# Written order in all of pass 1 of a two-layer graph kernel, with operand calls in two batches of three

## Chip, cores and metric

The kernel runs on one core of a Trainium2 chip. Its time is the device time of one execution in microseconds (us): median 2493.08 of three runs (2492.97 to 2498.91). A core has five engines that run side by side: TensorE (PE in the profile, with its weight loads as PEld) for matrix products into PSUM, VectorE (DVE), ScalarE (ACT) and GpSimd (POOL) for work on rows of elements, and SyncE (SP), which here issues transfers. Each works through its own queue of instructions and waits for semaphores of the others.

## What is computed

Two graph layers over 128 graphs of 64 nodes with 768 features each. Pass 1 of the kernel is layer 0; pass 2, an attention layer, is not touched by the change.

```python
# --- layer 0 ---
h = relu(layernorm(x))                              # x: 128 x 64 x 768
ctx  = (adj   @ (h @ Wadj.T)) / max(deg, 1)         # adj: 0/1, 64 x 64 per graph
ctx += (adj.T @ (h @ Wrev.T)) / max(rdeg, 1)
ctx += h @ Wself.T                                  # biases left out here
rel  = agg  @ Wr.T      # agg[i]  = sum over j of adj[i,j] * E[rels[i,j]]
rel += ragg @ Wrr.T     # the same over the transposed graph
x = x + ctx + rel
# --- layer 1: (graph attention), input relu(layernorm(x)) ---
```

## The kernel before

The 8192 rows are worked through as 32 pairs (p) of 128-row tiles (k = 0, 1). The three weight products of layer 0 are joined into one 3 x 3 block product, done for pairs 1 to 31 with 15 instead of 18 (as in fast matrix multiplication), so sums of blocks have to be formed: `form` makes sums f1 to f11 of the operand blocks a00 to a12, and `weights_sums` sums g and u, v, w of the weight blocks, once. Each product has 6 matmuls (12 instructions, since f32 goes in two), and its PSUM bank a, b, c or d is read by VectorE after it:

```python
PRODUCTS = (       # operand, weight, bank, first in bank, block of x, sign, with counts
    ("f1", "g6", "a", True, "11", "+", False),
    ("f7", "g10", "b", True, "00", "-", False),
    ("a01", "b11", "d", True, "01", "+", True),
    ("f4", "b21", "a", False, "01", "-", False),
    ("a00", "g12", "b", False, "01", "-", False),
    ("f3", "g8", "c", True, "12", "-", False),
    ("a02", "g14", "a", False, "00", "-", False),
    ("f9", "g9", "b", False, "02", "+", False),
    ("f11", "b10", "d", True, "00", "+", True),
    ("f6", "g5", "a", False, "02", "+", False),
    ("f8", "g3", "b", False, "12", "-", False),
    ("f10", "b12", "c", False, "02", "+", True),
    ("f5", "b22", "a", False, "12", "-", False),
    ("a11", "g1", "b", False, "11", "+", True),
    ("f2", "g11", "a", False, "10", "+", True),
)
...
psw = px.enter_context(tc.tile_pool(name="psw0", bufs=1, space=bass.MemoryType.PSUM))  # pwa to pwd
pss = px.enter_context(tc.tile_pool(name="pss0", bufs=2, space=bass.MemoryType.PSUM))  # pb: two
...
            def product(an, bn, b, first, c, sign, cnt):
                def step(q, s):
                    if first and q == s == 0:
                        new(b)                       # bank[b] = psw.tile([P, 512], F32, name=f"pw{b}")
                    nc.tensor.matmul(bank[b][:, :CQ], OPS[p, an][:, q, s, :], bw[bn][...], ...)
                    if q == KQ - 1 and s == 2 and c:
                        if cnt:
                            counts(b, c)             # two bf16 matmuls on the table of relations
                        add(b, c, sign)              # VectorE: x += or -= bank
                ...                                  # 6 steps a product
            for x in PRODUCTS if p else PLAIN:       # 90 steps a pair
                product(*x)
            rest_of = ["12"] if p else ["00", "10"]  # counts alone, bank d, and its add
```

What the next pair needs is made beside the products of this one: `merged(main(p), side)` puts each side step ahead of the product step whose number it has. `operands` makes one operand block: 4 matmuls (8 instructions, 64 rows each) into a `pb` buffer of two banks, one for each graph of the tile, and a copy to SBUF. `count_t` turns the counts of relations by TensorE, through the same `pb` buffers.

```python
        def count_t(p, k):
            ...
            for i, (a, b) in enumerate(PARTS):
                nc.tensor.transpose(pn[: 3 * (b - a), i, :], ..., identb)
                nc.scalar.copy(cn[: 3 * (b - a), i, :], pn[: 3 * (b - a), i, :])

        def operands(p, k, q):
            t = 2 * p + k
            ps = pss.tile([P, GT, 512], F32, name="pb")
            for i in range(2):
                kb = 2 * q + i
                for g in range(GT):
                    s = slice(g * N, (g + 1) * N)
                    nc.tensor.matmul(ps[:, g, i * 3 * N : (i + 1) * 3 * N],
                                     H0[t][s, kb * P : (kb + 1) * P],
                                     rts[p % 2][s, k].rearrange("p s n -> p (s n)"), ...)
            a = OPS[p, f"a{k}{q}"] = ...             # SBUF, 128 x 768 f32
            nc.scalar.copy(a.rearrange("p h s (g n) -> p g (h s) n", g=GT),
                           ps[:, :, : 6 * N].rearrange("p g (x n) -> p g x n", n=N))
```

The side steps, with the engine that has most of the work: `prep`, `prep_c`, `ids_worth`, `ids_sum`, `digits` (VectorE: the counts of relations), `devs` or `deviation` (VectorE: mean and variance, then a power on GpSimd), `degrees` (one matmul) with a reciprocal and two products on VectorE, `finish` (the end of the pair before: statistics; then mean, ScalarE's relu, GpSimd's sum, three stores), `load` (SyncE).

Up to and with pair 1's stretch the instructions of each engine are kept in the order in which the program writes them (`manual_schedule`, in the variable `written`). For pairs 2 to 31 they are not: the tile scheduler places them.

```python
        second = [                                   # beside pair 1, for pair 2
            (0, lambda: form(1, "f5", "f6", "f3")), (7, lambda: prep(2)),
            (7, lambda: weights_sums("g9")), (10, lambda: form(1, "f10")),
            (13, lambda: devs(2)), (18, lambda: form(1, "f11")),
            (20, lambda: degrees_and_norms(2)), (25, lambda: weights_sums("g1")),
            (30, lambda: prep_c(2)), (32, ends[0]), (37, lambda: ids_worth(2, 0)), (40, ends[1]),
            (43, lambda: ids_sum(2, 0)),
            (46, lambda: operands(2, 1, 2)), (46, lambda: operands(2, 1, 1)),
            (49, ends[2]), (53, lambda: form(2, "f1")), (55, ends[3]),
            (56, lambda: ids_worth(2, 1)),
            (58, lambda: operands(2, 0, 0)), (58, lambda: operands(2, 0, 2)),
            (61, lambda: ids_sum(2, 1)), (64, lambda: digits(2)),
            (66, lambda: form(2, "f7", "f4")), (66, lambda: load(3)), (74, row_constants),
            (70, lambda: operands(2, 1, 0)), (70, lambda: operands(2, 0, 1)),
            (77, lambda: form(2, "f8", "f9", "f2")),
            (80, lambda: count_t(2, 0)), (85, lambda: count_t(2, 1))]
        for p in range(NP):
            if p < 2:
                more = (first, second)[p]
            else:                                    # own: f5 f6 f3, f10, f11; side: as above
                more = own(p) + side(p + 1) + [(3, ...finish(p - 1, k)...)]
            if p == NP - 1:
                more += fetch()                      # weights of pass 2: loads and sums
            merged(main(p), more)
            if p == 1:
                written.close()
```

Of the kernel before, what the change touches and what calls it, by code (L numbers as in the profile page):

```python
# [8 lines left out]
F32 = mybir.dt.float32  # L9
# [6 lines left out]
P = 128  # L16
# [116 lines left out]
def kernel(  # L133
# [45 lines left out]
    nc = tc.nc  # L179
# [56 lines left out]
            step()  # L236

    in_order = {mybir.EngineType.PE, mybir.EngineType.DVE, mybir.EngineType.Activation,  # L240
                mybir.EngineType.Pool}
    written = ctx.enter_context(ExitStack())
# [33 lines left out]
                a = c * HB + i * H  # L276
                nc.sync.dma_start(dl[a : a + H, :], ident[0:H, 0:H])

    def deviation(src, to, mv, behind=False):

        st = small.tile([P, 2, 6], F32, name="st")
        for i in range(2):
            ins = nc.vector.bn_stats(st[:, i, :], src[:, i * HALF : (i + 1) * HALF])  # L283
            if behind and i == 0:
                tc.keep_in_program_order(ins)
        nc.vector.bn_aggr(mv, st.rearrange("p a b -> p (a b)"))
        ve = small.tile([P, 1], F32, name="ve")
        nc.vector.tensor_scalar(ve, mv[:, 1:2], EPS, None, op0=OP.add)  # L288
        nc.gpsimd.tensor_tensor(to[:, 0:1], ve, mhalf, op=OP.pow)  # L289

    def scaled_mean(to, mv):

        nc.vector.scalar_tensor_tensor(to[:, 1:2], mv[:, 0:1], -1.0, to[:, 0:1],
                                       op0=OP.mult, op1=OP.mult)

    def stats(src, to, behind=False):
        mv = small.tile([P, 2], F32, name="mv")
        deviation(src, to, mv, behind)
        scaled_mean(to, mv)

# [59 lines left out]
    with ExitStack() as px:  # L362
# [126 lines left out]
        def relu(t, to):  # L489
            h = H0[t] = work.tile([P, D], F32, name="h0")  # L490
            nc.scalar.activation(h, X[t], AF.Relu, scale=to[:, 0:1], bias=to[:, 1:2])

        def norm(t):
            to = small.tile([P, 2], F32, name="rn")
            stats(X[t], to, behind=(t // 2 == 3))
            relu(t, to)

        def prep(p):

            af = ADF[p] = work.tile([P, 2, 2, N], F32, name="af", bufs=1)  # L500
            ins = nc.vector.tensor_copy(af, AI[p])
            if p == 3:
                tc.keep_in_program_order(ins)
            ab = AB[p] = work.tile([P, 2, 2, N], BF16, name="ab", bufs=1)
            nc.vector.tensor_copy(ab, af)

# [21 lines left out]
        def degrees(p):  # L528


            ds = pss.tile([P, 2, 512], F32, name="pb")[:, 0, : 4 * N].rearrange(
                "p (k d n) -> p k d n", k=2, d=2)
            nc.tensor.matmul(ds, blkb, AB[p], start=True, stop=True)
            rd = work.tile([P, 2, 2, N], F32, name="rd", bufs=1)
            nc.vector.tensor_scalar(rd, ds, 1.0, None, op0=OP.max)
            return rd

        def one_over(rd):
            nc.vector.reciprocal(rd, rd)

        def over_degrees(p, rd):

            for d in range(2):
                nc.vector.tensor_mul(rts[p % 2][:, :, 1 - d, :], ADF[p][:, :, d, :], rd[:, :, d, :])
# [16 lines left out]
        def count(p, k):  # L561
            ids_worth(p, k)
            ids_sum(p, k)
# [17 lines left out]
        def count_t(p, k):  # L581
            c3 = CT_T[p, k]
            pn = pss.tile([P, 2, 512], F32, name="pb")[:, 0, :P].bitcast(BF16).rearrange(
                "p (i n) -> p i n", i=2)
            cn = CT_T[p, k] = work.tile([P, 2, P], BF16, name="cntT", bufs=4)
            for i, (a, b) in enumerate(PARTS):
                nc.tensor.transpose(pn[: 3 * (b - a), i, :],  # L587
                                    c3[:, a:b, :].rearrange("p v c -> p (v c)"), identb)
                nc.scalar.copy(cn[: 3 * (b - a), i, :], pn[: 3 * (b - a), i, :])

        def operands(p, k, q):


            t = 2 * p + k
# [7 lines that stand above are left out]
                                     rts[p % 2][s, k].rearrange("p s n -> p (s n)"),  # L602
                                     start=True, stop=True)

            a = OPS[p, f"a{k}{q}"] = (
                work.tile([P, KQ, 3, P], F32, name="oq") if (k, q) == (1, 1) else
                work.tile([P, KQ, 3, P], F32, name="op", bufs=17))
            nc.scalar.copy(a.rearrange("p h s (g n) -> p g (h s) n", g=GT),  # L608
                           ps[:, :, : 6 * N].rearrange("p g (x n) -> p g x n", n=N))

        def form(p, *names):

# [72 lines left out]
            mv = small.tile([P, 2], F32, name="mv")  # L685
            return (lambda: deviation(X[t], to, mv), norm_and_store)

        def degrees_of(p):
            rd = degrees(p)
            one_over(rd)  # L690
            over_degrees(p, rd)

        def side(p):

            if p >= NP:
                return []
            return [(24, lambda: load(p + 1)),
                    (0, lambda: (prep(p), prep_c(p))),
                    (0, lambda: norm(2 * p)),
                    (0, lambda: norm(2 * p + 1)),  # L700
                    (9, lambda: degrees_of(p)),
                    (15, lambda: count(p, 0)),
                    (30, lambda: count(p, 1)),
                    (40, lambda: digits(p)),
                    (46, lambda: operands(p, 1, 2)),
                    (46, lambda: operands(p, 1, 1)),
                    (51, lambda: form(p, "f1")),
                    (58, lambda: operands(p, 0, 0)),
                    (58, lambda: operands(p, 0, 2)),
                    (64, lambda: form(p, "f7", "f4")),  # L710
                    (70, lambda: operands(p, 1, 0)),
                    (70, lambda: operands(p, 0, 1)),
                    (76, lambda: form(p, "f8", "f9", "f2")),
                    (80, lambda: count_t(p, 0)),
                    (80, lambda: count_t(p, 1))]

        def own(p):

            return [(0, lambda: form(p, "f5", "f6", "f3")),
                    (10, lambda: form(p, "f10")),  # L720
                    (18, lambda: form(p, "f11"))]

        def deviations(ts):
# [40 lines left out]
        def weights_sums(*names):  # L766
# [16 lines left out]
            (23, lambda: prep(1)),  # L783
            (24, lambda: devs(1)),
            (26, lambda: table_part(2)),
            (28, lambda: degrees_and_norms(1)),
            (30, lambda: weights_sums("w", "v")),
            (36, lambda: weights_sums("g6")),
            (38, lambda: weights_sums("u", "g14")),
# [18 lines left out]
            (91, lambda: form(1, "f8", "f9", "f2")),  # L808
            (92, lambda: count_t(1, 1))]

        ends = [f for k in range(2) for f in finish(0, k)]
        second = [
            (0, lambda: form(1, "f5", "f6", "f3")),
            (7, lambda: prep(2)),
            (7, lambda: weights_sums("g9")),
            (10, lambda: form(1, "f10")),
            (13, lambda: devs(2)),
            (18, lambda: form(1, "f11")),
            (20, lambda: degrees_and_norms(2)),
            (25, lambda: weights_sums("g1")),  # L820
            (30, lambda: prep_c(2)),
            (32, ends[0]),
            (37, lambda: ids_worth(2, 0)),
            (40, ends[1]),
            (43, lambda: ids_sum(2, 0)),
            (46, lambda: operands(2, 1, 2)),
            (46, lambda: operands(2, 1, 1)),
            (49, ends[2]),
            (53, lambda: form(2, "f1")),
            (55, ends[3]),  # L830
            (56, lambda: ids_worth(2, 1)),
            (58, lambda: operands(2, 0, 0)),
            (58, lambda: operands(2, 0, 2)),
            (61, lambda: ids_sum(2, 1)),
            (64, lambda: digits(2)),
            (66, lambda: form(2, "f7", "f4")),
            (66, lambda: load(3)),
            (74, row_constants),
            (70, lambda: operands(2, 1, 0)),
            (70, lambda: operands(2, 0, 1)),  # L840
            (77, lambda: form(2, "f8", "f9", "f2")),
            (80, lambda: count_t(2, 0)),
            (85, lambda: count_t(2, 1))]
        for p in range(NP):
            if p < 2:
                more = (first, second)[p]
            else:
                more = own(p) + side(p + 1) + [
                    (3, lambda: [f() for k in range(2) for f in finish(p - 1, k)])]
            if p == NP - 1:  # L850
                more += fetch()
            merged(main(p), more)
            if p == 1:
                written.close()


    with ExitStack() as px:
# [432 lines left out]
```

## Time and profile before

| | |
|---|---|
| time, median of 3 runs | 2493.08 us |
| span of the profiled execution, granted TensorE clock | 2493.3 us, 0.996 |
| pass 1, first product to last counts | 14.5 to 1502 us |
| one pair of pass 1, from pair 4 on | 45.95 us |
| one product (12 instructions of 128 x 256 f32) | 2.59 us |
| ScalarE's copy of an operand block, 128 x 768 | 0.80 us |
| VectorE's sum of two operand blocks, 128 x 768 | 0.95 us |

How to read it: a group line names the source line, engine and operation, then output and inputs by their names in the program, shapes, and how many there were, then busy time and the mean of one, and what the engine waited for before. In a timeline each row is start, duration, engine, line and operation, and in brackets the idle time before with what ended it. PE's instructions overlap, so the distance of two starts is the step, not the duration.

### The profile page before, as it was taken

To read this page: it belongs to the slowest core of one execution; us is meant where nothing else is said; L and a number is where in the kernel's file an instruction comes from. 1 tells how busy PE (TensorE), PEld (TensorE's weight loads), DVE (VectorE), ACT (ScalarE), POOL (GpSimd) and SP (SyncE) were. 2 spreads that over 40 slices of the span, in tenths; PEclk is the share of its full clock that TensorE was granted. 3 is DMA by queue.
4 is the path that set the end of the run, shared out by engine and by line. 5 is a ranking of instruction groups with operands and counts; after the bars stand their busy time and mean duration, and the time that the engine had idled before them with its cause. 6 is when DMAs were issued, how large, how long until landed. Compare 5 with 4: busy or idle time off the path is not lost. (4 is left out here: it accounts for less than half of the span.)

```text
span 2493.3 us, 35434 instructions
## 1 busy us (share of the span) xinstructions
PE 2462.6 (99%) x12108; PEld 1727.9 (69%) x12108; DVE 1972.4 (79%) x4105; ACT 1075.8 (43%) x3591; POOL 441.5 (18%) x799
## 2 busy tenths in 40 slices
PE   8999999999999999999999999999999999999997
PEld 6878888888888888888888884444444444444445
DVE  8887777777776776777777655888888888888888
ACT  2222222222222222222222214777777777777777
POOL 1121121121221211211211101111111111111122
PEclk9999999999999999999999999999999999999998
DMA  5121131121121221211211234444444444444434
GB/s 178 59 106 53 53 106 53 54 106 53 67 93 54 82 77 53 99 61 53 106 54 51 102 133 133 102 109 107 105 110 104 104 104 109 111 104 104 109 85 96
DMA packets 116215, 224.58 MB, mean 90 GB/s; under 512 B 36554, under 2 KB 49981, under 8 KB 116034
## 3 DMA queue, kind: packets, MB, share of 16 engines
q1 hardware_dynamic: 106162, 197.50, 24.2%
q0 software_dynamic: 9728, 24.78, 6.3%
q8 instruction: 95, 1.56, 0.3%
q14 instruction: 86, 0.70, 0.1%
q10 hardware_dynamic: 144, 0.04, 0.0%
HBM read 96.07 MB, written 100.66 MB: 79 GB/s over the span
## 5 line engine op out<-in xcount | busy, mean ns | idle before, releaser
L647 PE MATMUL pwa<-weights,op 128*128 128x256 f32 x2304 | 542.6, 383 | 1.9 <-DVE x L639 1.5
L647 PEld LDWEIGHTS pwa<-weights,op 128*128 128x128 f32 x2304 | 422.9, 190 | 71.2 <-DVE x L639 9.2
L608 ACT COPY op<-pb 128x768 f32<-128x768 f32 x160 | 124.0, 797 | 734.4 <-PE pb L600 734.4
L647 PE MATMUL pwb<-weights,op 128*128 128x256 f32 x1536 | 368.9, 381 | 0.3 <-DVE x L639 0.3
L315 DVE TENSOR_TENSOR op<-op 128x768 f32<-128x768 f32 x248 | 231.3, 953 | 149.7 <-ACT op L608 149.5
L647 PEld LDWEIGHTS pwb<-weights,op 128*128 128x128 f32 x1536 | 284.5, 190 | 46.7 <-issue 7.2
L943 PE MATMUL pma<-weights,op_f 128*128 128x512 f32 x620 | 307.7, 593 | 0.3 <-DVE weights L970 0.3
L995 ACT ACTIVATE pr<-pr 128x128 f32<-128x128 f32 x768 | 225.3, 296 | 25.2 <-DVE pr L985 25.2
L943 PE MATMUL pmb<-weights,op_f 128*128 128x512 f32 x372 | 191.2, 595 | 0.0
L289 POOL TENSOR_TENSOR rn<-ve,mhalf 128x1 f32<-128x1 f32 x128 | 106.7, 834 | 470.8 <-DVE ve L288 467.2
L943 PEld LDWEIGHTS pma<-weights,op_f 128*128 128x128 f32 x620 | 111.8, 190 | 112.9 <-issue 104.3
L647 PE MATMUL pwc<-weights,op 128*128 128x256 f32 x780 | 187.4, 383 | 1.3 <-DVE op L315 1.3
L647 PE MATMUL pwd<-weights,op 128*128 128x256 f32 x768 | 176.3, 379 | 0.0
L647 PEld LDWEIGHTS pwc<-weights,op 128*128 128x128 f32 x780 | 145.5, 190 | 27.9 <-issue 7.2
L579 POOL COPY c<-cnt 128x243 bf16<-128x243 bf16 x64 | 47.8, 775 | 636.9 <-PE pb L587 590.7
L647 PEld LDWEIGHTS pwd<-weights,op 128*128 128x128 f32 x768 | 145.8, 190 | 20.0 <-issue 0.2
L283 DVE BATCH_NORM_STATS2 st<-x 128x6 f32<-128x384 f32 x256 | 134.0, 546 | 31.9 <-DMA x<-in_x_dram 30.5
L600 PE MATMUL pb<-r,h 64*128 64x192 f32 x1536 | 151.6, 336 | 0.0
L677 ACT ACTIVATE hf<-x,rn 128x768 f32<-128x768 f32 x64 | 65.8, 1028 | 194.5 <-issue 125.3
L600 PEld LDWEIGHTS pb<-r,h 64*128 64x128 f32 x1536 | 122.7, 187 | 33.5 <-issue 32.3
L995 ACT ACTIVATION_READ_ACCUMULATOR pr<-pr 128x1 f32 x768 | 144.3, 188 | 0.0
L679 POOL TENSOR_TENSOR x<-x,hf 128x768 f32<-128x768 f32 x64 | 116.7, 1824 | 98.5 <-ACT hf L677 98.5
(207 smaller groups left out, 4278.9 us busy)
## 6 DMA issues: line engine op xcount, KB each, us to landing
x<-in_x_dram SPq DMA_DIRECT2D x64, 384.0 KB
h<-hf SPq DMA_DIRECT2D x64, 384.0 KB
out_dram<-x SPq DMA_DIRECT2D x64, 384.0 KB
hh<-hh SPq DMA_DIRECT2D x64, 384.0 KB
h<-h SPq DMA_DIRECT2D x64, 384.0 KB
x<-hh SPq DMA_DIRECT2D x64, 384.0 KB
out_dram<-f POOLq DMA_DIRECT2D x62, 384.0 KB, 5.1
hx<-weights SPq DMA_DIRECT2D x88, 192.0 KB
```

The costliest lines, as they stand in the source:

```text
L283: ins = nc.vector.bn_stats(st[:, i, :], src[:, i * HALF : (i + 1) * HALF])
L289: nc.gpsimd.tensor_tensor(to[:, 0:1], ve, mhalf, op=OP.pow)
L315: return (nc.vector.tensor_add if s1 == "+" else nc.vector.tensor_sub)(to, x, y)
L579: nc.gpsimd.tensor_copy(c3, CNT[p][:, k, :, None].to_broadcast([P, NROW, 3]))
L600: nc.tensor.matmul(ps[:, g, i * 3 * N : (i + 1) * 3 * N], H0[t][s, kb * P : (kb + 1) * P], rts[p % 2][s, k].rearrange("p s n -> p (s n)"), ...
L608: nc.scalar.copy(a.rearrange("p h s (g n) -> p g (h s) n", g=GT), ps[:, :, : 6 * N].rearrange("p g (x n) -> p g x n", n=N))
L647: nc.tensor.matmul(bank[b][:, :CQ], OPS[p, an][:, q, s, :], bw[bn][:, (s * KQ + q) * CQ : (s * KQ + q + 1) * CQ], start=(first and q == s ...
L677: nc.scalar.activation(h, X[t], AF.Relu, scale=to[:, 0:1], bias=to[:, 1:2])
L679: nc.gpsimd.tensor_add(X[t], X[t], h)
L943: nc.tensor.matmul(bank[p, b], OPS[p, an][:, q, :], bw2[bn][:, 2 * q * CQ : 2 * (q + 1) * CQ], start=(first and q == 0), stop=(q == KQ - 1 ...
L995: nc.scalar.activation(PR[t][:, j, h, :], PR[t][:, j, h, :], AF.Copy, accum_out=to)
```

## The change

All of pass 1 is written in order, so that no pair's instructions are placed by the scheduler: one list `beside(p)`, in the manner of `second`, serves pairs 1 to 31, and `written` closes after the last. The six operand calls of a pair go in two batches of three (steps 50 and 67) instead of three batches of two (46, 58, 70), so that TensorE leaves its products twice and not three times. Since there are two `pb` buffers, the third call of a batch needs the first one's again; the first copy of each batch is therefore cut in two, half on ScalarE and half on VectorE. `count_t` has both transposes ahead of both copies. In pair 0's stretch the degrees of pair 1 move from step 28 to 34. Helpers that are used no more go.

```diff
@@ count_t
             for i, (a, b) in enumerate(PARTS):
                 nc.tensor.transpose(pn[: 3 * (b - a), i, :],
                                     c3[:, a:b, :].rearrange("p v c -> p (v c)"), identb)
+            for i, (a, b) in enumerate(PARTS):
                 nc.scalar.copy(cn[: 3 * (b - a), i, :], pn[: 3 * (b - a), i, :])
 
-        def operands(p, k, q):
+        def operands(p, k, q, shared=False):
...
-            nc.scalar.copy(a.rearrange("p h s (g n) -> p g (h s) n", g=GT),
-                           ps[:, :, : 6 * N].rearrange("p g (x n) -> p g x n", n=N))
+            a = a.rearrange("p h s (g n) -> p g (h s) n", g=GT)
+            ps = ps[:, :, : 6 * N].rearrange("p g (x n) -> p g x n", n=N)
+            if shared:
+                nc.scalar.copy(a[:, 0], ps[:, 0])
+                nc.vector.tensor_copy(a[:, 1], ps[:, 1])
+            else:
+                nc.scalar.copy(a, ps)
... (own, side and their helpers go)
@@ first
-            (28, lambda: degrees_and_norms(1)),
+            (34, lambda: degrees_and_norms(1)),
... (ends and second go)
+        def beside(p):
+            ends = [f for k in range(2) for f in finish(p - 1, k)]
+            steps = [(0, lambda: form(p, "f5", "f6", "f3")), (10, lambda: form(p, "f10")),
+                     (18, lambda: form(p, "f11"))]
+            steps += list(zip((28, 36, 46, 55), ends))
+            if p == 1:
+                steps += [(8, lambda: weights_sums("g9")), (25, lambda: weights_sums("g1")),
+                          (74, row_constants)]
+            if p + 1 == NP:
+                return steps + fetch()
+            n = p + 1
+            return steps + [
+                (7, lambda: prep(n)),
+                (13, lambda: devs(n)),
+                (20, lambda: degrees_and_norms(n)),
+                (30, lambda: prep_c(n)),
+                (37, lambda: ids_worth(n, 0)),
+                (43, lambda: ids_sum(n, 0)),
+                (50, lambda: operands(n, 1, 2, True)),
+                (50, lambda: operands(n, 1, 1)),
+                (50, lambda: operands(n, 0, 0)),
+                (54, lambda: form(n, "f1")),
+                (56, lambda: ids_worth(n, 1)),
+                (60, lambda: ids_sum(n, 1)),
+                (64, lambda: digits(n)),
+                (66, lambda: load(n + 1)),
+                (67, lambda: operands(n, 0, 2, True)),
+                (67, lambda: operands(n, 1, 0)),
+                (67, lambda: operands(n, 0, 1)),
+                (71, lambda: form(n, "f7", "f4")),
+                (77, lambda: form(n, "f8", "f9", "f2")),
+                (80, lambda: count_t(n, 0)),
+                (85, lambda: count_t(n, 1))]
+
         for p in range(NP):
-            if p < 2:
-                more = (first, second)[p]
-            else:
-                more = own(p) + side(p + 1) + [
-                    (3, lambda: [f() for k in range(2) for f in finish(p - 1, k)])]
-            if p == NP - 1:
-                more += fetch()
-            merged(main(p), more)
-            if p == 1:
-                written.close()
+            merged(main(p), beside(p) if p else first)
+        written.close()
```

More of the change, by code (lines that the diff above doesn't have):

```diff
@@ L277, in row_constants, with deviation @@
                 nc.sync.dma_start(dl[a : a + H, :], ident[0:H, 0:H])
-    def deviation(src, to, mv, behind=False):
+    def deviation(src, to, mv):
         st = small.tile([P, 2, 6], F32, name="st")
         for i in range(2):
-            ins = nc.vector.bn_stats(st[:, i, :], src[:, i * HALF : (i + 1) * HALF])
-            if behind and i == 0:
-                tc.keep_in_program_order(ins)
+            nc.vector.bn_stats(st[:, i, :], src[:, i * HALF : (i + 1) * HALF])
         nc.vector.bn_aggr(mv, st.rearrange("p a b -> p (a b)"))
@@ L294, in scaled_mean @@
                                        op0=OP.mult, op1=OP.mult)
[L296 to L299, printed above, removed]
     PL = 3 * KQ * CQ
@@ L491, in relu @@
             nc.scalar.activation(h, X[t], AF.Relu, scale=to[:, 0:1], bias=to[:, 1:2])
[L493 to L496, printed above, removed]
         def prep(p):
             af = ADF[p] = work.tile([P, 2, 2, N], F32, name="af", bufs=1)
-            ins = nc.vector.tensor_copy(af, AI[p])
-            if p == 3:
-                tc.keep_in_program_order(ins)
+            nc.vector.tensor_copy(af, AI[p])
             ab = AB[p] = work.tile([P, 2, 2, N], BF16, name="ab", bufs=1)
@@ L686, in finish @@
             return (lambda: deviation(X[t], to, mv), norm_and_store)
[L688 to L721, printed above, removed]
         def deviations(ts):
@@ L809 @@
             (92, lambda: count_t(1, 1))]
[L811 to L843, printed above, removed]
```

## The prediction, made before the change was run

> **What bounds the kernel now.** I read the page's shares first, then cut pass 1 into stretches from one pair's first product to the next (an answer by windows: length, then busy time and instructions of PE, PEld, DVE, ACT, POOL, then granted clock, DMA share, GB/s), then read timelines inside a stretch.
>
> ```profile
> PE 2462.6 (99%) x12108; PEld 1727.9 (69%) x12108; DVE 1972.4 (79%) x4105; ACT 1075.8 (43%) x3591; POOL 441.5 (18%) x799
> ...
> 14.49:76.68 62.19, 58.56 (x320) 48.63 (x318) 54.36 (x77) 15.70 (x26) 6.75 (x7) 1.00 0.41 131
> 76.68:124.92 48.24, 46.60 (x249) 39.24 (x248) 44.46 (x91) 11.20 (x16) 8.51 (x8) 1.00 0.22 76
> 124.92:171.77 46.85, 46.14 (x245) 38.21 (x243) 43.95 (x101) 13.19 (x18) 9.04 (x12) 1.00 0.20 71
> 171.77:221.11 49.34, 47.88 (x245) 40.09 (x246) 35.13 (x78) 11.13 (x16) 9.08 (x9) 0.97 0.19 67
> 221.11:267.06 45.95, 45.95 (x247) 38.79 (x246) 34.10 (x75) 11.13 (x16) 8.54 (x8) 1.00 0.20 72
> ...
> 818.46:864.41 45.95, 45.95 (x248) 38.78 (x246) 34.17 (x75) 11.13 (x16) 8.54 (x8) 1.00 0.21 72
> ```
>
> Pass 1 lasts to 1502 us and is bound by TensorE. The first row is pair 0, the second pair 1, both already in written order; then two stretches of transition to the scheduler's order; from pair 4 on every stretch is 45.95 us with PE never idle, VectorE busy 34.2 of it. So written order has little to win per pair, and it can lose. Three details decide (timeline of PE, and one line each of DVE and ACT; start, duration, count at the end):
>
> ```profile
> 799.72 0.38 PE L647 MATMUL pwa<-weights,op 128*128 128x256 f32 x1
> 800.03 1.57 PE L600 MATMUL pb<-r,h 64*128 64x192 f32 x16
> 801.53 1.13 PE L647 MATMUL pwa<-weights,op 128*128 128x256 f32 x4
> ...
> 818.01 0.39 PE L631 MATMUL pwa<-tab,cntT 126*128 126x256 bf16 x2
> 818.24 0.39 PE L631 MATMUL pwd<-tab,cntT 126*128 126x256 bf16 x2
> 818.46 0.60 PE L647 MATMUL pwb<-weights,op 128*128 128x256 f32 x2
> 818.91 2.86 PE L647 MATMUL pwa<-weights,op 128*128 128x256 f32 x12
> ...
> 818.44 0.42 DVE L639 TENSOR_TENSOR x<-pwa,x 128x256 f32<-128x256 f32 x1
> ...
> 839.84 0.80 ACT L608 COPY op<-pb 128x768 f32<-128x768 f32 x1 [13.93 <-PE pb L600]
> ```
>
> A batch of two operand calls is 16 instructions. At a pair's end the two f7 instructions (pwb) stand ahead of the new pair's f1 (pwa): VectorE is just then emptying bank pwa, 818.44 to 818.86. And losses of the two written pairs and the transition:
>
> ```profile
> 32.64 0.28 PE L533 MATMUL pb<-ab,blkb 128*128 128x256 bf16 x1 [2.00 <-DVE ab L505]
> ...
> 117.09 0.22 PE L587 MATMUL pb<-identb,c 128*126 128x128 bf16 x1
> 117.67 0.22 PE L587 MATMUL pb<-identb,c 128*117 128x128 bf16 x1 [0.35 <-ACT cntT L589]
> ...
> 121.67 0.70 PE L647 MATMUL pwc<-weights,op 128*128 128x256 f32 x2 [1.29 <-DVE op L315]
> ...
> 173.93 4.54 PE L647 MATMUL pwa<-weights,op 128*128 128x256 f32 x12 [1.46 <-DVE x L639]
> ```
>
> **What the Trainium skill says.** "PSUM — Partial Sum Buffer", section Engine vs sequencer instructions: VectorE and ScalarE take their queue strictly first in, first out, and matmuls start in program order. The timelines agree: nothing overtakes, so a late VectorE instruction ahead of a wanted copy delays the copy, and a matmul that waits for a bank delays all behind it. Same page, PSUM bank collisions: two engines may not be in one bank (and quadrant) at once, different banks are free. That is why the second transpose at 117.67 waits for ScalarE's copy, and why the shared copy is cut at the bank. "TensorE: Matmul & The Clock Gate", Part 1: after an idle window of about 3.4 us the array runs at half rate for about as long. Here the stretch with the 1.46 us wait shows it: clock 0.97, and 12 products in 4.54 us where 2.75 is usual; the 2.00 us wait at 32.64 shows none, so it is a matter of luck.
>
> **Part 1, one batch fewer (gain).** From 799.72 to 800.03 is 0.31 us where a product's step is 0.216 (12 in 2.59, as 2.75 less the overlap), so entry costs 0.09. The batch takes 800.03 to 801.53, 1.50 us; a single call in pair 0 (8 instructions) takes 0.85, so 8 more cost 0.65, and 16 without the exit would be 1.30: exit 0.20. The first product after it is late by another 0.10 (next one 0.32 later, 0.216 usual; four show 1.13 where 1.03 is usual). Each interruption costs 0.39 us. Three become two: **-0.39 us a pair**.
>
> **Part 2, f1 behind the bank (loss).** In written order nothing stands between the last counts (pwd at 818.24 and 818.35) and f1, which would start at 818.46. It writes pwa, one buffer, which the sum at 818.44 frees at 818.86; with some 0.05 us of signal it starts at 818.91: 0.45 us of waiting against 0.02 now. **+0.43 us a pair.** VectorE can't do it sooner: its input, the counts at 818.01, ends then.
>
> **Part 3, the third call of a batch waits for its PSUM slot (loss).** There are two pb slots; the third call takes the first one's. The first copy starts 0.97 us after the batch (838.87 to 839.84, also 110.95 to 111.92). Whole on ScalarE it takes 0.80 and frees the slot at 1.82 with the signal; shared, 384 elements on each: ScalarE 0.48 (a copy of that size in pass 2), VectorE about 0.55 (an estimate between 0.42 for 256 and 0.68 for 512 elements from PSUM in this trace), so the slot is free at 1.57. Two calls last 1.30, so the wait is **at least 0.27 us in each batch**, and longer where VectorE is late. I laid VectorE's queue out in written order from the durations of pair 1's timeline. From the end of product 1 (its sum 0.33) to the shared copy of the first batch stand: four statistics calls (2 x 1.36 and, for the pair that ends, 2 x 1.36), six more sums (2.0), f11 0.86, degrees 0.34, two means 0.13, reciprocal 1.78, its two products 0.41, digits' preparation 2.32, the other mean 0.1, ids_worth 2.0, ids_sum 1.82: 17.5 us with the first sum. TensorE needs from there to the first copy's start 38 steps of 0.432 + counts, degrees and entry 0.4 + 0.97 - 0.2 = 17.6. So VectorE arrives just in time: 0.27. From the end of product 8 to the second batch: three sums 1.0, f1 0.86, mean 0.1, ids_worth 2.0, ids_sum 1.82, digits 0.8 = 6.57 against 6.48: wait 0.36. Together 0.63. An error of the layout costs when VectorE is late and gains nothing when it is early. **+0.63 us a pair**, and 0.85 would not surprise me.
>
> **Part 4, count transposes.** Both transposes first, then both copies: in the scheduler's pairs they are hidden already (two groups of two), so about 0 there; in pair 0 four and in pair 1 one such wait (about 0.46 each, one 0.69) go: -2.5 us once.
>
> **Part 5, once.** Degrees moved from step 28 to 34, 2.6 us later on PE: the 2.00 us wait goes, -2.0. The transition goes: 1.3 in pair 1, 46.85 - 45.95 = 0.9 and 49.34 - 45.95 = 3.4: -5.6. Against that: in pair 1's stretch VectorE still has the weight sums g9 and g1 (1.7 us each) and starts about 1 us late, since TensorE reaches it sooner; its first shared copy then comes some 4 us late, TensorE waits as long (+4), and the clock may drop (+1.7). Sum about -4.4. The last pair's weight loads come behind two store groups in SyncE's order; its TensorE work is 40.3 us, VectorE has room, and I put 0.
>
> **Sum.** Per pair -0.39 + 0.43 + 0.63 = +0.67, times 30 pairs (1 to 30) = +20; once -4.4; 2493 + 20 - 4.4 = 2508.7, so **2508 us**.
>
> **The rivals.** First, the waits are hidden or VectorE is earlier than laid out: each batch at 0.27 or less. Then the pairs cost +0.2 to +0.6 or nothing, and the once-only gains carry it: 2485 to 2495. For it speaks that VectorE is idle some 10 us of each 45.95; against it that the copy can't start before 0.97. Second, in-order VectorE becomes the bound: it waits at every sum for a bank with ready work behind it. VectorE's 34.2 us plus 0.9 for the shared copies fits 46 only if the waits don't add up; if each batch waits 1.5 us and the clock drops, a pair takes 48 and the kernel 2550. Against it speaks pair 1, which kept within about 0.1 us of 45.95 once its named waits are taken off (48.24 less 0.43 for the two pwc instructions that belong to the next pair, less 1.3 and 0.46, is 46.05), with 3.4 us more VectorE work, but with two calls a batch. Third, transfers in written order: load(n+1) is issued at step 66 behind the stores, and used 10 us later; SyncE's own waits show none above 2.1 us but for the relu, so I expect nothing.
>
> **Range and chances.** The waits of part 3 are the open term: 30 pairs times 0.3 to 1.3 us in all moves the sum by 30 us. Eight in ten: 2492 to 2527. A gain over 2% would need 1.6 us off each pair of a saturated engine: 0.01. A loss over 2% needs +1.8 us a pair: 0.04. Within: 0.95.
>
> **What would show it.** Right: pairs 4 to 30 at 46.4 to 46.9 us; f1's first matmul with some 0.4 us idle ahead of it, released by the sum (the line of today's L639); two batches of 24 with a gap ahead of the last 8, released by the shared copies; no wait ahead of the second transpose; no half-rate stretch at 174. Wrong: pairs under 45.95 (the third call doesn't wait), or gaps elsewhere in PE, at forms or sums.

## The result, and the profile after

The changed kernel takes 2539.14 us (median of four runs, 2536.9 to 2540.7) against 2495.88 before: ratio 1.0173, 95% interval 1.0154 to 1.0191. It is slower by 1.7%, which lies outside the predicted range. Spans of single profiles in this document can differ by some 4 to 6 us for one reason alone, how long the array's first work ran at half rate (first product at 14.4 to 15.0 or at 18.2 to 18.6 us); so stretches of pass 1 are compared, not spans.

The shares of the page first. PE is at 97% instead of 99%: a saturated engine has got gaps.

```profile
PE 2468.2 (97%) x12108; PEld 1730.2 (68%) x12108; DVE 2013.3 (79%) x4165; ACT 1068.2 (42%) x3591; POOL 429.0 (17%) x799
```

Next the same windows, one pair of pass 1 in each (length, then busy time and instructions of PE, PEld, DVE, ACT, POOL, granted clock, DMA share, GB/s): pair 0, pair 1, pair 2, a pair from the middle, and the last pair.

```profile
14.48:73.26 58.78, 57.90 (x320) 48.42 (x319) 54.43 (x77) 15.22 (x26) 8.32 (x7) 1.00 0.43 137
73.26:121.02 47.76, 46.04 (x248) 38.74 (x246) 39.65 (x82) 10.89 (x16) 7.92 (x8) 1.00 0.20 71
121.02:168.50 47.48, 46.15 (x245) 38.85 (x246) 35.52 (x76) 10.89 (x16) 7.87 (x8) 1.00 0.20 70
833.26:880.75 47.49, 46.15 (x246) 38.86 (x246) 35.53 (x76) 10.89 (x16) 7.88 (x8) 1.00 0.20 70
1498.03:1547.20 49.17, 44.22 (x198) 37.30 (x198) 29.85 (x45) 4.22 (x6) 6.51 (x6) 0.93 0.55 185
```

The last pair before:

```profile
1461.76:1502.08 40.32, 40.32 (x194) 34.88 (x193) 22.50 (x35) 3.89 (x4) 4.13 (x3) 1.00 0.61 205
```

The transition is gone and pair 0 is 3.4 us shorter, but every pair takes 47.48 us where the scheduler's took 45.95. The last one takes 48.7 where it took 40.3: its last counts end at 1546.70, and the window above runs 0.5 us beyond them. (From here on a last pair is counted to the end of its last counts; the recorded expectations start from 49.2.) By stretches: pair 0 -3.4; pair 1 -0.5; pair 2 +0.6; pair 3 -1.9; pairs 4 to 30, 27 times 1.53, +41.3; pair 31 +8.4. Sum +44.5, and the two profiles differ by 2537.7 - 2493.3 = 44.4.

Where a pair loses it (PE's timeline, in brackets the idle time with what ended it), a boundary of pairs, the first batch of three, and the end of pass 1:

```profile
833.26 2.86 PE L638 MATMUL pwa<-weights,op 128*128 128x256 f32 x12 [0.29 <-DVE x L630]
...
854.43 1.03 PE L638 MATMUL pwd<-weights,op 128*128 128x256 f32 x4
855.38 1.57 PE L586 MATMUL pb<-r,h 64*128 64x192 f32 x16
857.47 0.92 PE L586 MATMUL pb<-r,h 64*128 64x192 f32 x8 [0.52 <-DVE op L598]
858.32 1.99 PE L638 MATMUL pwd<-weights,op 128*128 128x256 f32 x8
...
1540.99 5.43 PE L638 MATMUL pwa<-weights,op 128*128 128x256 f32 x12 [4.58 <-DVE x L632]
```

f1, the first product of a pair, waits for its bank, as predicted. The batch of three lasts 858.32 - 855.38 = 2.94 us; without a wait it would be 2.15 (16 instructions 1.50, eight more 0.65, as in the prediction), so the third call costs 0.79 us; the second batch (866.09 to 869.03) has the same 2.94. The bracket shows only 0.52 of it: instructions overlap, and the loads of weights start late too. The two rows for the copies that the third call waits for, on ScalarE and on VectorE:

```profile
856.35 0.48 ACT L597 COPY op<-pb 128x384 f32<-128x384 f32 x1 [3.78 <-PE pb L586]
```

```profile
855.89 0.41 DVE L630 TENSOR_TENSOR x<-pwb,x 128x256 f32<-128x256 f32 x1
856.86 0.56 DVE L598 COPY op<-pb 128x384 f32<-128x384 f32 x1 [0.56 <-ACT op L597]
```

ScalarE's half starts 0.97 us after the batch's start, as laid out. VectorE is free by then, also as laid out, but it starts only at 856.86, 0.03 us after ScalarE's half has ended at 856.83. The halves run one after the other.

### The profile page after: what moved, and what is told of

Its sections match the earlier page's. It is cut to its first block, busy times and chain, and to the rows that moved or that the text cites. A ratio compares the mean times of both kernels' runs of the same rounds, so it can differ in the third digit from the quotient of the medians.

```text
span 2537.7 us, 35495 instructions
## 1 busy us (share of the span) xinstructions
PE 2468.2 (97%) x12108; PEld 1730.2 (68%) x12108; DVE 2013.3 (79%) x4165; ACT 1068.2 (42%) x3591; POOL 429.0 (17%) x799
## 5 line engine op out<-in xcount | busy, mean ns | idle before, releaser
L638 PE MATMUL pwb<-weights,op 128*128 128x256 f32 x1536 | 352.8, 379 | 0.0
L638 PEld LDWEIGHTS pwb<-weights,op 128*128 128x128 f32 x1536 | 291.5, 190 | 40.0 <-DVE x L630 0.4
L483 ACT ACTIVATE h<-x,rn 128x768 f32<-128x768 f32 x64 | 62.3, 1019 | 400.6 <-DVE rn L290 381.7
L286 POOL TENSOR_TENSOR rn<-ve,mhalf 128x1 f32<-128x1 f32 x128 | 74.0, 578 | 888.2 <-DVE ve L285 866.9
L670 POOL TENSOR_TENSOR x<-x,hf 128x768 f32<-128x768 f32 x64 | 156.7, 2449 | 311.6 <-ACT hf L668 311.6
L586 PE MATMUL pb<-r,h 64*128 64x192 f32 x1536 | 159.8, 340 | 31.6 <-DVE op L598 30.7
L638 PE MATMUL pwd<-weights,op 128*128 128x256 f32 x768 | 184.3, 383 | 0.0
L894 PE MATMUL pmc<-weights,op_f 128*128 128x512 f32 x248 | 129.7, 605 | 0.2 <-DVE weights L923 0.2
```

The source lines that it names most:

```text
L586: nc.tensor.matmul(ps[:, g, i * 3 * N : (i + 1) * 3 * N], H0[t][s, kb * P : (kb + 1) * P], rts[p % 2][s, k].rearrange("p s n -> p (s n)"), ...
L670: nc.gpsimd.tensor_add(X[t], X[t], h)
L894: nc.tensor.matmul(bank[p, b], OPS[p, an][:, q, :], bw2[bn][:, 2 * q * CQ : 2 * (q + 1) * CQ], start=(first and q == 0), stop=(q == KQ - 1 ...
```

## The experiments

Two theories were set against each other: the two halves of a shared copy are ordered by the program (1), or VectorE comes late because its queue is in written order (2). A third (3) is for the last pair.

### No shared copy: e1_whole

```diff
-                (50, lambda: operands(n, 1, 2, True)),
+                (50, lambda: operands(n, 1, 2)),
-                (67, lambda: operands(n, 0, 2, True)),
+                (67, lambda: operands(n, 0, 2)),
```

> Both batches of three stay, no copy is shared: ScalarE makes each whole. Theory 1 (the two halves run one after the other, VectorE's only after ScalarE's, so that sharing costs): the slot comes free 0.97 + 0.80 + 0.05 us after the batch's start, against 2.09 now (855.38 to 857.47), so the third call comes 0.27 us sooner in each batch; a pair 47.48 - 0.54 = 46.9 us, 16 us less in all: 2523. Theory 2 (sharing as such works, VectorE is only late): the whole copy is no better than the shared one, pair 47.5 or more, 2539 or more.

Measured: 2523.4 us, ratio to before 1.0115 (1.0095 to 1.0135); a pair 46.94. The batch, ScalarE's whole copy and the third call:

```profile
852.09 1.57 PE L586 MATMUL pb<-r,h 64*128 64x192 f32 x16
...
853.05 0.80 ACT L600 COPY op<-pb 128x768 f32<-128x768 f32 x1 [3.78 <-PE pb L586]
...
853.90 0.92 PE L586 MATMUL pb<-r,h 64*128 64x192 f32 x8 [0.25 <-ACT op L600]
```

The third call comes 1.81 us after the batch's start instead of 2.09. One copy of 0.80 on one engine beats two of 0.48 and 0.56 that follow each other. So the sharing in the change is a loss in itself, 0.54 us a pair.

### Which tile orders the halves: e2_scratch and e8_tiles

Both halves write to interleaved 64-column pieces of one SBUF tile, and both read one PSUM tile of two banks. In e2_scratch VectorE's half goes out of PSUM into a tile of its own and then to its place:

```diff
-                nc.vector.tensor_copy(a[:, 1], ps[:, 1])
+                half_b = work.tile([P, KQ * 3 * N], F32, name="hb", bufs=1)
+                hv = half_b.rearrange("p (x n) -> p x n", n=N)
+                nc.vector.tensor_copy(hv, ps[:, 1])
+                nc.vector.tensor_copy(a[:, 1], hv)
```

> The shared copy stays, but VectorE's half goes first to a tile of its own and then, by a second VectorE copy in SBUF, to its place between ScalarE's pieces. Theory 1a (the halves are put one after the other because they write interleaved 64-column pieces of one SBUF tile): the two copies out of PSUM start together at 0.97 us, the slot is free at 0.97 + 0.56 + 0.05 = 1.58, so the third call comes 0.5 us sooner in each batch: pair 46.5 us, 2509. Theory 1b (they are ordered because they read one PSUM tile): VectorE still starts when ScalarE ends, pair 47.5. Theory 2 (VectorE late by its queue): pair 47.5 too, with VectorE busy up to the copy.

Measured: 2539.6 us, ratio 1.0176 (1.0154 to 1.0198), a pair 47.48 as in the change. VectorE's three rows in question and ScalarE's:

```profile
855.77 0.41 DVE L633 TENSOR_TENSOR x<-pwb,x 128x256 f32<-128x256 f32 x1
...
856.23 0.48 ACT L597 COPY op<-pb 128x384 f32<-128x384 f32 x1 [3.77 <-PE pb L586]
856.74 0.56 DVE L600 COPY hb<-pb 128x384 f32<-128x384 f32 x1 [0.55 <-ACT op L597]
```

VectorE now writes elsewhere, is idle for 0.55 us, and still waits for ScalarE. That rules out the SBUF tile as the sole reason, and theory 2 as well: VectorE's queue was free. So e8_tiles gives each graph's half a PSUM tile of its own:

```diff
-            ps = pss.tile([P, GT, 512], F32, name="pb")
+            ps = [pss.tile([P, 512], F32, name=f"pb{g}") for g in range(GT)]
... (matmuls to ps[g]; the shared halves read ps[0] and ps[1])
-                nc.scalar.copy(a, ps)
+                for g in range(GT):
+                    nc.scalar.copy(a[:, g], ps[g])
... (table products, degrees and count transposes: one such tile, or two)
```

> The change, but each operand call has two PSUM tiles of one bank in place of one tile of two, and a whole copy is two ScalarE copies. If theory 1b holds (the halves of a shared copy are ordered because both read one tile): VectorE's half starts beside ScalarE's, at 0.97 us, the slot is free at 1.58 and the third call comes 0.5 us sooner in each of two batches; pair 46.6 us, 2513. If something else orders them (VectorE's and ScalarE's writes to one SBUF tile as well, or PSUM as a whole): 47.5.

Measured: 2517.1 us, ratio 1.0077 (1.006 to 1.0093), a pair 46.64.

```profile
842.60 2.52 PE L587 MATMUL pb<-r,h 64*128 64x192 f32 x24
...
843.55 0.48 ACT L598 COPY op<-pb 128x384 f32<-128x384 f32 x1 [3.76 <-PE pb L587]
843.60 0.56 DVE L599 COPY op<-pb 128x384 f32<-128x384 f32 x1
```

Now the halves run side by side, and the batch takes 845.05 - 842.60 = 2.45 us instead of 2.94. In the second batch VectorE starts 0.20 us later than ScalarE (853.96 against 853.76) and the batch takes 2.59. The two gains, 0.49 and 0.35, are the whole 0.84 us of the pair. Theory 1 stands, and its reason is settled: what was ordered are two reads of one PSUM tile, though in different banks. Both halves still write to one SBUF tile here, so that tile orders nothing. The Trainium skill ("PSUM — Partial Sum Buffer", Specifications) says that ScalarE and VectorE can be in PSUM in parallel as long as banks don't collide; e8_tiles shows it on this chip. It was a semaphore that the program has for two accesses to one tile, not the hardware, that put them in a row.

### Three batches of two in written order: e3_three

```diff
-                (50, lambda: operands(n, 1, 2, True)),
-                (50, lambda: operands(n, 1, 1)),
-                (50, lambda: operands(n, 0, 0)),
-                (54, lambda: form(n, "f1")),
+                (46, lambda: operands(n, 1, 2)),
+                (46, lambda: operands(n, 1, 1)),
+                (53, lambda: form(n, "f1")),
+                (58, lambda: operands(n, 0, 0)),
+                (58, lambda: operands(n, 0, 2)),
-                (67, lambda: operands(n, 0, 2, True)),
-                (67, lambda: operands(n, 1, 0)),
-                (67, lambda: operands(n, 0, 1)),
-                (71, lambda: form(n, "f7", "f4")),
+                (66, lambda: form(n, "f7", "f4")),
+                (70, lambda: operands(n, 1, 0)),
+                (70, lambda: operands(n, 0, 1)),
```

> Written order in all of pass 1 as in the change, but three batches of two operand calls at steps 46, 58 and 70, none shared. If the waits for the third call are the loss (2 x 0.79 us a pair) and the third interruption costs 0.39: pair 47.48 - 1.58 + 0.39 = 46.3 us, 30 pairs, 2503. If written order as such is the loss (VectorE in order behind each sum), the pair stays above 47 us and 2530.

Measured: 2503.0 us, ratio 1.0032 (1.002 to 1.0043). The window of one pair:

```profile
912.77:959.07 46.30, 46.01 (x245) 38.80 (x245) 34.95 (x74) 11.24 (x16) 8.66 (x8) 1.00 0.20 72
```

46.30 is within a hundredth what the terms give (47.48 - 2 x 0.79 + 0.39 = 46.29). Written order as such costs nothing on VectorE; the third interruption is cheaper than two waits for a buffer.

### f7 ahead of f1: e4_f7

```diff
-            for x in PRODUCTS if p else PLAIN:
+            for x in PRODUCTS[1::-1] + PRODUCTS[2:] if p else PLAIN:
```

> The change, with products f7 and f1 of pass 1 swapped, so that a pair begins in bank b and not in the bank that VectorE is just emptying. If f1's wait is all there is at the boundary: 0.45 us less a pair, 47.03, 30 boundaries, 2526. Rival: the sums come later then and the wait moves to another bank: pair 47.3 to 47.5.

Measured: 2528.3 us, ratio 1.0134 (1.0113 to 1.0154). In this kernel the last pair's f1 product reads in part weights of pass 2, since their load at step 7 now stands ahead of its last steps; the pairs before it are as in the change, and show:

```profile
918.74:965.66 46.92, 45.88 (x247) 38.85 (x246) 35.53 (x76) 10.88 (x16) 7.91 (x8) 1.00 0.20 71
```

0.56 us less a pair: the wait of 0.45 and 0.10 of slow first step after it. So f1's wait was all there was at the boundary. The two profiles differ by only 2537.7 - 2524.6 = 13.1 us, less than 30 times 0.56, since the last pair grew by 3.1 us. It is what the Trainium skill asks for ("Perfetto Trace Analysis", Optimizing Tensor Performance): independent groups should rotate through PSUM banks, so that one is emptied beside the next group's matmuls.

### The last pair: e5_last, e6_all, e10_best

In e5_last, the ends of pair 30 are early beside pair 31:

```diff
-            steps += list(zip((28, 36, 46, 55), ends))
+            steps += list(zip((28, 36, 46, 55) if p + 1 < NP else (6, 10, 14, 18), ends))
```

> The change, but beside the last pair the ends of the pair before (statistics, relu, stores) go at steps 6, 10, 14 and 18 instead of 28, 36, 46 and 55. Theory 3 (in SyncE's order the weight loads of pass 2 stand behind stores that wait for those ends, VectorE waits in order for the last load, and the last product waits for a sum behind it): the last pair falls from 49.2 to 41 us, the kernel by 8, to 2531; the 4.58 us wait ahead of the last product and the half-rate stretch go. Rival (the loads themselves are too slow, or in-order VectorE has too much to do there): 0 to 2 us.

Measured: 2534.9 us, ratio 1.0144 (1.0126 to 1.0161). The last pair takes 45.2 us instead of 48.7, less than half of the gain that was expected. The 4.58 us wait is gone, but the stores now stand ahead of all weight blocks but the first in SyncE's order, VectorE waits 6.06 and 7.00 us for blocks, and two earlier products wait 2.23 and 1.44 us for sums behind these weight sums. e6_all takes this together with e3_three and e4_f7's swap, with the first block's load at step 13 so that it comes behind f1.

> Written order in all of pass 1 with three batches of two calls, f7 ahead of f1, and the early ends of e5_last; the first weight block of pass 2 is loaded at step 13. If the named losses are all: pair 46.30 - 0.55 = 45.75 (e4_f7 took 0.55 off a pair), 30 of them 16.5 us off e3_three's 2503, and 7 to 8 off the last pair: 2479, 0.6% under the kernel before. If the last pair's loss comes back in other clothes (as with f7 first, where it grew by 3): 2485 to 2490.

Measured: 2485.6 us, ratio 0.9953 (0.9939 to 0.9967): the pairs at 45.74 as expected, the last at 47.6. There VectorE waited 7.31 and 6.47 us for weights. So e10_best puts the ends behind the first loads, and the later sums behind their landing:

```diff
+            steps += list(zip((28, 36, 46, 55) if p + 1 < NP else (24, 30, 36, 42), ends))
-                    (22, "g10"), (28, "g6"), (41, "g12"), (46, "u"), (50, "g14"), (57, "w"),
-                    (59, "g5"), (65, "v"), (67, "g3"), (70, "g9"), (73, "g1"), (76, "g8"),
-                    (79, "g11"))])
+                    (22, "g10"), (28, "g6"), (45, "v"), (50, "g12"), (54, "u"), (56, "g14"),
+                    (64, "w"), (66, "g5"), (78, "g3"), (80, "g9"), (82, "g1"), (84, "g8"),
+                    (86, "g11"))])
```

> As e6_all, but beside the last pair the ends stand at steps 24, 30, 36 and 42, behind the first three weight blocks in SyncE's order, and VectorE's later weight sums stand 4 to 12 steps later, when their blocks have landed. Theory 3 (a load behind stores, and VectorE in order behind the load): the last pair falls from 47.3 to 41 us, the kernel to 2479. Rival (another wait takes its place): 2483 or more.

Measured: 2481.1 us, ratio 0.9943 (0.9929 to 0.9957), last pair 41.3. In this kernel v at step 45 is written to a place that the last pair's product f6 still reads as weights; e12_best below has it after that. Theory 3 stands: a load behind stores, VectorE in order behind the load, TensorE behind a sum that VectorE holds back. Ends and sums moved together here, so what each is worth isn't shown.

### Two parts alone on the kernel before: e11_once

```diff
             for i, (a, b) in enumerate(PARTS):
                 nc.tensor.transpose(...)
+            for i, (a, b) in enumerate(PARTS):
                 nc.scalar.copy(...)
-            (28, lambda: degrees_and_norms(1)),
+            (34, lambda: degrees_and_norms(1)),
```

> The kernel before with two parts of the change alone: both count transposes ahead of both copies, and the degrees of pair 1 at step 34. Pair 0's stretch falls by 3.4 us (62.2 to 58.8, as in the change), pair 1's by some 0.5; pairs 4 to 30 of the scheduler stay at 45.95 or 45.9: 2489, 0.2% under before. If the transposes matter in every pair: 45.87 a pair, 2487.

Measured: 2492.8 us, ratio 0.9988 (0.9979 to 0.9998). Pair 0 is at 58.78 as expected and pair 1 at 45.73, 2.5 us less where 0.5 was expected, but most of it is lost again behind them: the next two stretches are 49.45 and 49.21 (before 46.85 and 49.34), and each of the scheduler's pairs takes 46.05, 0.10 more. The written part gained 5.9 us and the scheduler's part behind it gave back 5.2; why its pairs got longer was not tried apart.

### A version that beats both: e12_best

e10_best with `v` at step 68, thus: all of pass 1 in written order, three batches of two, f7 ahead of f1, and the last pair's loads, ends and sums placed as above.

> As e10_best, with the weight sum v at step 68 in place of 45 (its place in SBUF holds g5 of pass 1 until step 59). Theory 3: last pair 41 us, kernel 2480 to 2481, 0.5% under before. Rival: v's later step moves a wait ahead of pass 2's first products: 2483 or more.

Measured: 2482.5 us, ratio 0.9945 (0.9931 to 0.996). The windows of pair 1, a middle pair and the last:

```profile
74.15:119.99 45.84, 45.84 (x245) 38.90 (x246) 38.11 (x77) 11.01 (x16) 8.66 (x8) 1.00 0.21 74
897.57:943.31 45.74, 45.74 (x247) 38.79 (x246) 34.95 (x74) 11.24 (x16) 8.64 (x8) 1.00 0.20 73
1446.45:1487.33 40.88, 40.31 (x192) 34.63 (x191) 25.06 (x41) 3.92 (x4) 5.59 (x4) 1.00 0.65 222
```

PE is busy without a gap in pairs 1 to 30. The last window ends 0.3 us ahead of the last counts; to their end the pair takes 41.15. Against the profile before, with a span 12.9 us longer, pair 0 gives 3.0 us, pairs 1 to 3 give 7.1, the 27 others 0.21 each, 5.7; the last pair costs 0.8. And the rival named beforehand came in part: pass 2's first product waits for a sum that stands behind VectorE's last weight sums,

```profile
1491.46 1.10 PE L894 MATMUL pmd<-weights,op_a 128*128 128x512 f32 x2 [2.30 <-DVE x L630]
```

and what follows pass 1 takes 992.8 us where it took 991.3 in e10_best and 991.2 before. The expected 2480 to 2481 us were missed by about that much.

## Why the prediction was wrong

**What held.** Part 2: f1's wait is there at every boundary from pair 1's end on: it starts 0.565 us after the last count matmul's start where 0.112 is usual, thus 0.45. Part 1: e3_three gives 0.40 us for an interruption, by subtraction (2 x 0.79 less the 47.48 - 46.30 = 1.18 that it gained). The layout of VectorE's queue held too: it is free 0.1 us before the first shared copy is wanted, and about 0.2 us late at the second.

**What failed: the size of part 3.** The step was "shared, 384 elements on each: ... so the slot is free at 1.57". It took the halves as side by side. They follow each other: the slot is free at 2.04 and the third call comes at 2.09 us, 0.79 after the two calls' 1.30. Predicted 0.63 us a pair, measured 2 x 0.79 = 1.58, a difference of 0.95, times 30 pairs 28.5 us: alone as large as the whole miss (2493.3 + 15.6 predicted against a span of 2537.7, 28.8). That it is just as large is luck: the other errors, below, are -5.3, +8.4 and -2.4 us and nearly cancel. I had cited that different banks are free, and took from it that the copies would overlap; whether the program's dependencies let them is another question. The profile before had a hint that I overlooked: in pass 2, ScalarE and VectorE each read one half of the tile pmb, and there too VectorE waits and starts 0.03 us after ScalarE ends.

```profile
1512.57 0.38 ACT L959 ACTIVATE weights<-pmb 128x256 f32<-128x256 f32 x1 [2.11 <-PE pmb L943]
```

```profile
1512.98 0.42 DVE L972 TENSOR_TENSOR weights<-weights,pmb 128x256 f32<-128x256 f32 x1 [1.58 <-ACT weights L959]
```

These halves lie in one bank, so the tile and the bank could not be told apart by it. e8_tiles, where the copies overlap, has 46.64 us a pair, and the predicted terms give 45.95 + 0.67 = 46.62; its two waits, 0.30 and 0.44 us, are 0.11 more than predicted, and the transposes (below) 0.08 less.

**What failed too: the last pair put at 0.** It cost 8.4 us. I looked at how long SyncE had waited in the scheduler's order, where the sums also move freely. In written order the load of b12 stands behind the stores of the ends, and the second of these waits for GpSimd's sum:

```profile
1527.62 2.50 POOL L670 TENSOR_TENSOR x<-x,hf 128x768 f32<-128x768 f32 x1 [6.56 <-ACT hf L668]
...
1530.16 0.34 SPq L671 DMA_DIRECT2D out_dram<-x  x1
...
1531.58 0.95 SPq L340 DMA_DIRECT2D weights<-in_hw_t_dram  x1
...
1535.52 2.48 DVE L307 TENSOR_TENSOR weights<-weights 128x1024 f32<-128x1024 f32 x2 [3.98 <-DMA weights<-in_hw_t_dram]
```

The block lands at 1535.5, VectorE waits for it 3.98 us, and a sum of x behind the weight sums holds the last product for 4.58 us, after which the array ran at half rate (12 instructions in 5.43 us).

**What was too dark: the once-only terms.** Put at -4.4, they came to -9.7: pair 0 -3.4, and pairs 1 to 3 together -6.3 against their pair's steady time. The 5.7 us for VectorE's lag in pair 1 did not come: VectorE was late as expected (its shared copy at 99.45), but the third call's wait there is ended by ScalarE's copy of the second call (0.90 us, released by ACT oq): it had been given the second call's buffer, and VectorE's copy was not in its way.

**What was small.** The transposes were not quite nothing in steady pairs: by the starts in PE's timelines the four of a pair with their slow steps after took 0.42 us, now 0.33, so some -0.08 a pair. With it the pair closes: 0.43 - 0.39 + 1.58 - 0.08 = 1.54, measured 1.53. Sum of all: 30 x 1.53 - 9.7 + 8.4 = 44.6 against 44.4. The prediction put the second transpose's wait at 117.67 down to the rule on banks; both transposes write one tile and one bank, so no run here tells which of the two ordered it.

**The rivals.** Hidden waits, the first, did not come. VectorE as the bound in order, the second, was not it: it named the size (waits of over a microsecond in each pair) but the wrong reason. The third, transfers in written order, did nothing in pairs 1 to 30, but it is what the last pair lost by.

## What to carry to other kernels

When a copy out of PSUM is to be shared by two engines, give each half a PSUM tile of its own and see in the timeline that the second start doesn't follow the first end; otherwise one whole copy on one engine frees the buffer sooner (third call 1.81 us after the batch's start here, against 2.09). When a saturated TensorE is interrupted for small work, compare the interruption (some 0.4 us here) with what a longer batch waits for in buffers: here, with two buffers, two calls a batch (46.30 us a pair) beat three even with the halves side by side (46.64). And when a scheduler's order is written down by hand, copy its small reorderings (here two instructions of another bank at the boundary), and treat the first and last rounds, where loads stand behind stores, as cases of their own.

## What the runs showed of the hardware

- The half rate after a gap is not a matter of its length alone. In the change, 4.58 us of idle time were followed by 12 instructions of a product in 5.43 us; in e5_last 2.23 and 1.44 us were followed by 2.86, close to the usual 2.75, while before the change 1.46 us were followed by 4.54. So an idle window of about 3.4 us, which the prediction cites, was not needed for it: the measurement decides here.
- GpSimd's sum of 128 x 768 took 1.81 us in the scheduler's order and 2.48 us in the change, where it stands beside VectorE's bf16 products and reductions. In the middle pairs no wait of TensorE's leads back to it; in the last pair it is part of the path (2.50 us, above). The cause was not tried apart.
- After waits of 0.02 to 2.23 us the first step of a run of products was 0.32 instead of 0.216 us, 0.10 us on top of each wait.
